# Two graph layers on one core: a shorter grouping, a loop that starts one batch sooner, a new order at the end, and indirect transfers two at a time

## The chip, the cores and the metric

The kernel runs on one core of one Trainium2 chip. The metric is the device time of one execution in microseconds. The kernel before took 1087.72 us in the median of three runs (1087.29 to 1098.17). The profile is of one further execution, which took 1089.15 us; its instructions span 1087.4 us.

## The reference

x is 32 batches of 512 nodes with 512 features, adj a 512 x 512 matrix with about five entries a row, its diagonal set, all values under 1. Everything is float32.

```python
# layer 0
h = relu(layernorm(x))
x = x + einsum('bmd,nm->bnd', h, adj) @ w0 + b0
# layer 1: attention with 8 heads, masked by adj
h = relu(layernorm(x))
q, k, v = h @ Wq + bq, h @ Wk + bk, h @ Wv + bv          # per head of 64
scores = q k^T / 8 + (1 - adj) * -1e9
x = x + softmax(scores) v @ Wo + bo
```

Since every entry of adj is under 1, the mask term is of the order of -1e8 and more, and it leaves one source for each row: the node at which adj is largest in that row. Layer 1 is then, for each row, a fixed linear map of one chosen node's h: z = h[idx] @ (Wv Wo) + (bv Wo + bo), and rows that choose the same node share it. The program tests on the chip that this holds, and has other branches if it doesn't.

## The kernel before, in words

**Preparation.** The first part of `gnn_two_layers` folds Wv and Wo into one matrix, transposes adj, finds each row's chosen node (`idx`), the nodes chosen at all (`used`, 332 of 512 here, so 336 rows are reserved), and computes layer 0's first product of batch 0. Then `single_path` runs.

**A batch.** A batch's rows lie in four chunks of 128 partitions. In iteration b of `run_phase` TensorE computes layer 0's second product of batch b (`layer0`, L632 or L495), then the aggregation of batch b+1, then layer 1's product of batch b-1 (`layer1`, L495). Most products are 2 x 2 block products in the seven-product form (`product`). The iteration has 21 steps: `put(batch, step, f)` hangs a piece of other work on a step, and the pieces of a step are emitted after the step's matmuls and ahead of the evacuation of their result. The order is written out by hand and each engine executes its part in that order. Between layers, h goes to HBM (`put_h`, to hs), comes back with unused rows left out (`get_h`, to hc), and is transposed on VectorE; z goes to HBM (`put_z`), and an indirect transfer with addition (`finish`, L462) gathers it onto x. SyncE's queue carries hs, hc and z. GpSimd's queue carries the indirect transfers.

**Dense and regrouped batches.** Batches up to FIRST = 5 are read in their natural order. Aggregation is a dense 512 x 512 product in the first iterations. In parallel, `Plan` computes an order of the nodes in which the adjacency is sparse by blocks: a quarter of the nodes forms a first block, whose rows may use every source, and the others form three groups of 128. A group's rows may only use sources in the group itself and at most 128 rows from elsewhere, which are gathered once more as "extra rows". `Plan.schedule` spreads this over the dense iterations: `pick_r` chooses the first block, and then each of three rounds counts links (`sources`, `known`, `reach`), scores the nodes (`key_1`, `clip`), ranks them (`rank_pe`) and takes the best into groups (`pick_1`, `pick_2`). `positions`, `place_onehot`, `slots`, `slot_onehot`, `lists` and `indices` turn the groups into index lists (`xi`, `gi`); `rows`, `turn`, `save_at`, `tables`, `tables_g` and `mask_g` rearrange adj; `look_1`, `save_pi`, `look_2`, `packed` make the list by which z is gathered. If no group needs more than 128 extra rows, the flag is set (L893's register test) and the remaining iterations run as the regrouped loop: `spread` in place of the dense aggregation (L608, L611 and L614: 1,280 columns for each of four feature blocks). Else they run dense.

**The regrouped loop on GpSimd's queue.** In iteration b, in this order: `load_x` of batch b+2, four gathers of 128 rows of 2 KB (step 0, L462, `x<-in_x_dram,xi`); `load_g`, three gathers of extra rows (step 4, `at<-in_x_dram,gi`), which wait until ScalarE has read the earlier extra rows; `finish` of batch b-2, four gathers with addition (step 7, `x<-z,pplace`), which wait for z's eight transfers; a memset for `layer1` (L713); and `store` of batch b-2, four scatters (step 14, L479, `out_dram<-x,xi`), each after its own gather has landed. `tc.declare_no_dep` (L484) states that the scatters touch different rows. x has five buffers, so each load waits for the scatter that read its buffer. ScalarE takes the statistics of the extra rows (`NormMore`, L920; the first ones by `lead`, a `NormAct`), VectorE those of x (L361, L362).

**The end.** Batch 31's layer 1 (`layer1_rows`) is computed by rows for all nodes, since nothing is left to overlap. `fetch` reads the z of batches 29 and 30 into free buffers (`sel`, `yT`), `add_z` adds and stores them.

Of the kernel before, what the change touches and what calls it, by code (L numbers as in the profile page):

```python
# [18 lines left out]
P = 128  # L19
# [389 lines left out]
def single_path(ctx: ExitStack, tc: tile.TileContext, x, adj, out, kept, room):  # L409
# [45 lines left out]
    def run_phase(batches, sparse, small, ps_m, ps_t):  # L455
# [4 lines left out]

        def gather(dst, rows, at, **more):
            return nc.gpsimd.indirect_dma_start(out=dst, out_offset=None, in_=rows,  # L462
                                                in_offset=bass.IndirectOffsetOnAxis(ap=at, axis=0), **more)
# [11 lines left out]
        def store_rows(b, c, eng):  # L475
            if natural(b):
                eng.dma_start(out[b, c * P:(c + 1) * P, :], X[b][:, c, :])
                return
            stored = nc.gpsimd.indirect_dma_start(  # L479
                out=out_rows, out_offset=bass.IndirectOffsetOnAxis(ap=plan.xi[:, b, c:c + 1], axis=0),  # L480
                in_=X[b][:, c, :], in_offset=None)
# [197 lines left out]
        def layer1_rows(b):  # L679
            for r in range(C):  # L680
# [7 lines left out]
                nc.vector.tensor_add(x_r, bank.rearrange("p (c q e) -> p q c e", q=4, c=4), x_r)  # L688
                store_rows(b, r, nc.sync)
                for i in range(2):  # L690
                    add_z(B - 3 + r // 2, 2 * (r % 2) + i, nc.sync if r < 2 else nc.scalar)
# [65 lines left out]
        for b in batches:  # L757
            todo = [[] for _ in range(21)]
# [4 lines left out]

            if folded and b == FIRST - 1:
                put(b + 2, 8, load_g)
                for j in range(3):
                    put(b + 2, 12 + j, lambda b, j: lead.stats(j), j)
            if sparse and b == FIRST:
                put(b + 1, 0, lambda b: lead.power())
                put(b + 1, 0, lambda b: lead.offset())  # L770
                for j in range(3):
                    put(b + 1, 1 + j, lambda b, j: lead.relu(j), j)
            if sparse:
                if b > FIRST:
                    put(b + 2, 0, load_x)
                put(b + 2, 4, load_g)
# [6 lines left out]
            put(b - 2, 15 if b == B - 1 else 7 if sparse and b < B else 1, fetch if b > B - 2 else finish)  # L783
            if b < 2:
                put(b + 2, 2 * b, load_x)
            if b > 0 and not sparse:
                put(b + 3, 15, load_x)
# [8 lines left out]
            for c, step in enumerate((1, 3, 9, 12) if b == 0 else (9, 10, 11, 12) if b == B - 2 else (14, 15, 17, 19)):  # L796
                put(b + 1, step, add_b0, c)
            if b < B:
                halves = [norm(X[b], h1_t, [2 * i, 2 * i + 1], Norm if b > 0 or i == 1 else NormAct) for i in range(2)]
# [30 lines left out]
            on_act = b == 0 or folded and not sparse and b < FIRST - 1  # L830
# [32 lines left out]
            if sparse and b == FIRST + 1:  # L863
                put(b, 2, lambda b: plan.look_1())
                put(b, 6, lambda b: plan.save_pi())
                put(b, 15, lambda b: plan.look_2())
# [699 lines left out]
```

## Time and profile before

| | |
|---|---|
| median of three runs | 1087.72 us (1087.29 to 1098.17) |
| profiled execution | 1089.15 us, span 1087.4 us |
| PE busy, weight loads busy | 1011.2 us (93%), 900.0 us (83%) |
| DVE, ACT, POOL busy | 810.1 us (74%), 581.0 us (53%), 564.2 us (52%) |
| software queue (GpSimd's) | 43,984 packets, 118.27 MB, 45.4% of 16 engines |
| hardware queue (SyncE's) | 115,760 packets, 83.37 MB, 30.0% of 16 engines |

How to read it: PE is TensorE, PEld its weight loads, DVE VectorE, ACT ScalarE, POOL GpSimd, SP SyncE. L462 is line 462 of the kernel before. A tile pair such as x<-z,pplace is what an instruction writes and reads. In a timeline, a bracket gives how long the engine was idle before the instruction and what released it; "issue" is a gap that no wait explains. An indirect transfer occupies POOL only while it is issued; the data land later.

The stages, by time in the span: preparation and batch 0 up to 70.93 us; dense iterations 1 to 4, 42.41, 38.90, 41.39 and 40.94 us; the start of the regrouped loop 107.86 us (234.57 to 342.43); 22 batches of the loop 669.68 us; the end 75.29 us.

### The profile page before, as it was taken

The numbers are of one execution on the slowest core, as the hardware profiler recorded it, in microseconds if no ns is written. First come the engines' busy times: TensorE is split into PE (matmuls) and PEld (weight loads), VectorE is DVE, ScalarE is ACT, GpSimd is POOL, SyncE is SP. The second block draws the span as 40 slices with busy tenths as digits, with TensorE's granted clock in tenths as the row PEclk, the third lists the DMA queues.
The fourth block names the chain that finished last, engine by engine and source line by source line (L and its number), as shares of the span: only waits on it lengthen the run. The fifth ranks groups of instructions, "written<-read, shape, count | busy, mean of one in ns | idle before, by whom it ended". The sixth has DMA issues, their size and how long they took to land.

```text
span 1087.4 us, 17059 instructions
## 1 busy us (share of the span) xinstructions
PE 1011.2 (93%) x5672; PEld 900.0 (83%) x5672; DVE 810.1 (74%) x1809; ACT 581.0 (53%) x1266; POOL 564.2 (52%) x659
## 2 busy tenths in 40 slices
PE   8999889978999889999999999999999998999993
PEld 7478778877898878999999988888889888999871
DVE  5897876857787658878777777778777776888762
ACT  3745345255555465566556556665555556666230
POOL 1023216646547435665575575555665565564326
PEclk9999999989899989999999999999999999999997
DMA  9244546968888768888888898988788787987654
GB/s 315 92 85 125 125 111 198 229 193 194 169 207 207 168 178 198 196 201 202 209 219 184 210 232 206 214 196 201 198 207 193 171 213 202 221 197 188 131 169 159
DMA packets 161314, 204.24 MB, mean 188 GB/s; under 512 B 17824, under 2 KB 105632, under 8 KB 161216
## 3 DMA queue, kind: packets, MB, share of 16 engines
q0 software_dynamic: 43984, 118.27, 45.4%
q1 hardware_dynamic: 115760, 83.37, 30.0%
q10 hardware_dynamic: 1472, 1.41, 0.4%
q8 instruction: 47, 0.77, 0.3%
q14 instruction: 51, 0.42, 0.1%
HBM read 120.66 MB, written 82.32 MB: 187 GB/s over the span
## 4 chain that ended last, share of the span: by engine, by line
PE 72%; ACT 4%; DVE 3%; issue 2%; POOL 2%; DMA 1%; another core or an unknown queue 1%; ACTq 0%; POOLq 0%; DVEq 0%
PE mm L495 51%; PE mm L611 11%; PE mm L614 6%; PE mm L608 2%; ACT zs L545 1%; POOL out_dram L479 1%; PE mm L685 1%; DVE st L361 1%; ACT h L379 1%; DMA x<-z,pplace 1%; DVE x L552 0%; DMA at<-in_x_dram,gi 0%; ACT h L394 0%; ACT yT L619 0%
## 5 line engine op out<-in xcount | busy, mean ns | idle before, releaser
L552 DVE TENSOR_TENSOR x<-mm,x 128x512 f32<-128x512 f32 x217 | 148.5, 685 | 130.2 <-PE mm L495 99.3
L379 ACT ACTIVATE h<-x,off,rstd 128x512 f32<-128x512 f32 x256 | 196.5, 807 | 7.8 <-DVE off L370 4.1
L365 ACT ACTIVATE rstd<-mv,eps 128x2 f32<-128x2 f32 (+1 forms) x91 | 26.6, 293 | 300.5 <-DVE mv L362 252.8
L495 PE MATMUL mm<-w_t,sel 128*128 128x256 f32 x744 | 176.1, 386 | 9.5 <-DVE x L552 9.4
L462 POOL DMA_INDIRECT x<-z,pplace x92 | 143.1, 1555 | 72.9 <-DMA z<-zr 37.4
L495 PEld LDWEIGHTS mm<-w_t,sel 128*128 128x128 f32 x744 | 142.1, 192 | 32.2 <-DVE x L552 12.7
L361 DVE BATCH_NORM_STATS2 st<-x 128x6 f32<-128x512 f32 x234 | 157.7, 674 | 1.1
L462 POOL DMA_INDIRECT at<-in_x_dram,gi x78 | 73.9, 948 | 162.0 <-ACT adjT L933 131.6
L495 PE MATMUL mm<-hTs,wvo_t 128*128 128x168 f32 x720 | 122.8, 317 | 32.3 <-ACT zs L545 31.0
L611 PE MATMUL mm<-ap,h 128*128 128x256 f32 x624 | 151.9, 380 | 0.0
L462 POOL DMA_INDIRECT x<-in_x_dram,xi x104 | 111.9, 1076 | 57.4 <-issue 27.1
L495 PEld LDWEIGHTS mm<-hTs,wvo_t 128*128 128x128 f32 x720 | 109.4, 196 | 38.6 <-ACT zs L545 37.3
L479 POOL DMA_INDIRECT out_dram<-x,xi x104 | 108.2, 1040 | 31.2 <-issue 22.0
L545 ACT ACTIVATE zs<-mm,cvo_c 128x168 f32<-128x168 f32 x240 | 82.8, 399 | 68.9 <-PE mm L495 50.9
L611 PEld LDWEIGHTS mm<-ap,h 128*128 128x128 f32 x624 | 110.6, 191 | 10.7
L495 PE MATMUL mm<-w_s,yT 128*128 128x256 f32 x496 | 118.5, 382 | 0.8 <-ACT zs L545 0.8
L495 PEld LDWEIGHTS mm<-w_s,yT 128*128 128x128 f32 x496 | 93.6, 192 | 12.7 <-ACT zs L545 1.0
L614 PEld LDWEIGHTS mm<-ag,adjT 128*128 128x128 f32 x624 | 86.0, 191 | 5.4
L614 PE MATMUL mm<-ag,adjT 128*128 128x128 f32 x624 | 86.4, 275 | 0.0
L586 DVE TENSOR_TENSOR x<-x,b_r 128x512 f32<-128x512 f32 x124 | 84.1, 679 | 0.0
L495 PE MATMUL mm<-hT,wvo 128*128 128x168 f32 x480 | 81.2, 314 | 0.0
L619 ACT COPY yT<-mm 128x512 f32<-128x512 f32 x104 | 59.8, 575 | 38.9 <-PE mm L614 30.3
(314 smaller groups left out, 1703.0 us busy)
## 6 DMA issues: line engine op xcount, KB each, us to landing
hc<-hs SPq DMA_DIRECT2D x124, 176.0 KB
z<-zr SPq DMA_DIRECT2D x120, 96.0 KB
z<-zr SPq DMA_DIRECT2D x120, 80.0 KB
hs<-h SPq DMA_DIRECT2D x50, 192.0 KB
hs<-h SPq DMA_DIRECT2D x50, 160.0 KB
out_dram<-x SPq DMA_DIRECT2D x24, 256.0 KB
x<-in_x_dram SPq DMA_DIRECT2D x16, 256.0 KB
x<-in_x_dram,xi POOLq DMA_INDIRECT x104
```

The costliest lines, as they stand in the source:

```text
L361: self.nc.vector.bn_stats(st, self.src[:, self.chunks[i], :])
L365: self.nc.scalar.activation(self.rstd[:, 0:len(self.chunks)], self.mv[:, :, 1], AF.Sqrt, bias=self.eps)
L379: self.nc.scalar.activation(dst, src, AF.Relu, bias=self.off[:, i:i + 1], scale=self.rstd[:, i:i + 1])
L462: return nc.gpsimd.indirect_dma_start(out=dst, out_offset=None, in_=rows, in_offset=bass.IndirectOffsetOnAxis(ap=at, axis=0), **more)
L479: stored = nc.gpsimd.indirect_dma_start(out=out_rows, out_offset=bass.IndirectOffsetOnAxis(ap=plan.xi[:, b, c:c + 1], axis=0), in_=X[b][:, ...
L495: nc.tensor.matmul(bank[:, m, 0:half], lhs[:, k, m * P:(m + 1) * P], rhs[:, k, :], start=(first and m == 0 and k == 0), stop=(k == 1), ski ...
L545: nc.scalar.activation(dst[:, m, :], bank[:, m, :], AF.Identity, bias=cvo_c[:, 2 * i + m:2 * i + m + 1])
L552: nc.vector.tensor_add(dst, bank, dst)
L586: nc.vector.tensor_add(X[b][:, c, :], X[b][:, c, :], b0_r)
L611: nc.tensor.matmul(two(bank, j), H0[b][:, j, cols], two(plan.ap[:, j, :], j), start=False, stop=False, skip_group_check=True)
L614: nc.tensor.matmul(bank[:, j * P:(j + 1) * P], extra[:, j - 1, cols], plan.ag[:, j - 1, j * P:(j + 1) * P], start=False, stop=(j == C - 1) ...
L619: nc.scalar.copy(yT[:, d, :], bank)
```

## The change

- `Plan.schedule` runs two rounds in place of three; the VectorE half of a count or ranking stands one step behind its TensorE half. The score (`key_1`, `clip`), the starting groups (`constants2`: every third node, in place of thirds of the partitions) and the constants that go with them differ; `positions` and `slot_onehot` are split into parts on several steps.
- FIRST is 4: the regrouped loop begins at iteration 4, and the steps of the plan, `load_g`, `lead` and `load_x` move with it. Plan steps that fall into the loop are issued from `plan.steps` too.
- In dense iterations 0 to 2 half of the second normalization's statistics are taken by ScalarE (`NormAct`).
- In `layer1_rows`, the adds and stores of batch 29 and the fetch of batch 30 come after the first row's product. The adds and stores of batch 30 follow the second and third rows.
- `paced` adds to every indirect transfer that the regrouped loop issues through `gather` and `store_rows`, in iterations below 30, a dependency on the completion of the last but one of them.

```diff
+        moved, pacing = [], [True]
+
+        def paced(move):
+            if sparse and pacing[0]:
+                if len(moved) > 1:
+                    tc.add_manual_dep(move.ins, moved[-2].ins.name, mybir.DependencyInfo(
+                        mybir.DependencyClass.Sync, mybir.DependencyReason.DATA), reason="two at a time")
+                moved.append(move)
+            return move
+
         def gather(dst, rows, at, **more):
-            return nc.gpsimd.indirect_dma_start(out=dst, out_offset=None, in_=rows,
-                                                in_offset=bass.IndirectOffsetOnAxis(ap=at, axis=0), **more)
+            return paced(nc.gpsimd.indirect_dma_start(out=dst, out_offset=None, in_=rows,
+                                                      in_offset=bass.IndirectOffsetOnAxis(ap=at, axis=0), **more))
...
-            stored = nc.gpsimd.indirect_dma_start(
+            stored = paced(nc.gpsimd.indirect_dma_start(
                 out=out_rows, out_offset=bass.IndirectOffsetOnAxis(ap=plan.xi[:, b, c:c + 1], axis=0),
-                in_=X[b][:, c, :], in_offset=None)
+                in_=X[b][:, c, :], in_offset=None))
...
+                if sparse and r == 0:
+                    for c in range(C):
+                        add_z(B - 3, c, nc.sync)
+                    fetch(B - 2)
                 store_rows(b, r, nc.sync)
                 for i in range(2):
-                    add_z(B - 3 + r // 2, 2 * (r % 2) + i, nc.sync if r < 2 else nc.scalar)
+                    if not sparse:
+                        add_z(B - 3 + r // 2, 2 * (r % 2) + i, nc.sync if r < 2 else nc.scalar)
+                    elif 0 < r < C - 1:
+                        add_z(B - 2, 2 * r - 2 + i, nc.sync)
...
+            pacing[0] = b < B - 2
...
             if folded and b == FIRST - 1:
-                put(b + 2, 8, load_g)
+                put(b + 2, 16, load_g)
+            if sparse and b == FIRST:
                 for j in range(3):
-                    put(b + 2, 12 + j, lambda b, j: lead.stats(j), j)
-            if sparse and b == FIRST:
-                put(b + 1, 0, lambda b: lead.power())
-                put(b + 1, 0, lambda b: lead.offset())
+                    put(b + 1, j, lambda b, j: lead.stats(j), j)
+                put(b + 1, 3, lambda b: lead.power())
+                put(b + 1, 3, lambda b: lead.offset())
                 for j in range(3):
-                    put(b + 1, 1 + j, lambda b, j: lead.relu(j), j)
+                    put(b + 1, 4 + j // 2, lambda b, j: lead.relu(j), j)
...
-                put(b + 2, 4, load_g)
+                put(b + 2, 6 if b == FIRST else 4, load_g)
...
+            on_act = b == 0 or folded and not sparse and b < FIRST - 1
             if b < B:
-                halves = [norm(X[b], h1_t, [2 * i, 2 * i + 1], Norm if b > 0 or i == 1 else NormAct) for i in range(2)]
+                halves = [norm(X[b], h1_t, [2 * i, 2 * i + 1], NormAct if i == 0 and (b == 0 or on_act) else Norm)
+                          for i in range(2)]
...
-FIRST = 5
+FIRST = 4
...
-        v.tensor_scalar(self.ind[:, 0:1], self.pp, 42.5, None, op0=ALU.is_lt)
-        v.tensor_scalar(self.ind[:, 2:3], self.pp, 85.5, None, op0=ALU.is_gt)
-        v.tensor_add(self.ind[:, 1:2], self.ind[:, 0:1], self.ind[:, 2:3])
-        v.tensor_scalar(self.ind[:, 1:2], self.ind[:, 1:2], -1.0, 1.0, op0=ALU.mult, op1=ALU.add)
+        for j in range(3):
+            v.tensor_reduce(self.ind[:, j:j + 1], self.kept["ident"][:, j::3], AX.X, ALU.add)
...
-        v.tensor_tensor(s, self.ps, self.ub, ALU.add)
-        v.scalar_tensor_tensor(s, s, 2.0, self.L[:, :, 0:3], op0=ALU.mult, op1=ALU.subtract)
+        v.scalar_tensor_tensor(s, self.ub, 1.5, self.ps, op0=ALU.mult, op1=ALU.add)
...
-        for r in range(3):
-            for gap, kind, f in ((0, pe, self.sources), (0, at, self.known), (3, pe, self.reach), (0, at, self.key_1),
-                                 (3, pe, self.rank_pe), (0, at, self.pick_1), (3, pe, self.rank_pe),
-                                 (0, at, self.pick_2), (3, None, None)):
-                k += gap
-                if f:
-                    kind(*divmod(k, 21), f)
+        for r in range(2):
+            for go, then in ((self.sources, self.known), (self.reach, self.key_1), (self.rank_pe, self.pick_1),
+                             (self.rank_pe, self.pick_2)):
+                pe(*divmod(k, 21), go)
+                at(*divmod(k + 1, 21), then)
+                k += 3
...
+        at(2, 18, self.rows)
+        at(2, 20, self.look_1)
         for m in range(4):
-            pe(*divmod(k + 10 + m, 21), self.turn, m)
-        at(*divmod(k + 12, 21), self.save_at, 0)
-        at(*divmod(k + 14, 21), self.save_at, 2)
-        at(3, 20, self.tables)
-        at(4, 0, self.tables_g)
-        at(4, 11, self.mask_g)
+            pe(3, 4 + m, self.turn, m)
+        at(3, 6, self.save_at, 0)
+        at(3, 8, self.save_at, 2)
+        at(3, 8, self.save_pi)
+        at(3, 12, self.tables)
+        at(3, 14, self.tables_g)
+        at(4, 0, self.mask_g)
+        at(4, 10, self.look_2)
+        at(5, 8, self.packed)
```

## The prediction

> **What bounds the kernel now.** I read the stretches of the profile first (columns: window, its length, then busy time and instruction count of PE, PEld, DVE, ACT and POOL, granted clock, DMA share, GB/s), to find the period of a batch in each stage.
>
> ```profile
> 113.34:152.24 38.90, 36.09 (x254) 31.70 (x253) 32.32 (x96) 17.10 (x39) 11.00 (x13) 1.00 0.59 146
> 193.63:234.57 40.94, 34.98 (x170) 31.57 (x168) 28.55 (x60) 16.22 (x37) 25.27 (x27) 0.92 0.86 219
> ...
> 342.43:1012.11 669.68, 644.47 (x3698) 593.18 (x3697) 513.05 (x1101) 395.03 (x858) 393.58 (x435) 0.99 0.84 199
> 1012.11:1087.40 75.29, 53.20 (x273) 41.95 (x271) 39.50 (x78) 16.72 (x36) 31.49 (x48) 0.91 0.55 161
> ...
> 530.91:559.76 28.85, 28.85 (x169) 26.67 (x168) 23.30 (x51) 17.90 (x39) 20.00 (x22) 1.00 0.83 215
> ```
>
> The first two are dense batches (2 and 4): 39 to 41 us each. The third is 22 batches of the regrouped loop, from the first L608 matmul of batch 8 to that of batch 30: 669.68/22 = 30.44 us each. The last is one undisturbed batch: TensorE has no gap, so 28.85 us is its floor, and 1.6 us a batch is lost on average to gaps. In the loop TensorE is the bound, with little to spare for a second bound.
>
> Next the queues, and then POOL's instructions over one undisturbed batch (start, us, what, idle before).
>
> ```profile
> q0 software_dynamic: 43984, 118.27, 45.4%
> q1 hardware_dynamic: 115760, 83.37, 30.0%
> ```
> ```profile
> 529.95 1.59 POOL L462 DMA_INDIRECT x<-z,pplace  x1 [3.89 <-DMA z<-zr]
> 531.85 1.55 POOL L462 DMA_INDIRECT x<-z,pplace  x1 [0.30 <-issue]
> ...
> 537.42 1.07 POOL L479 DMA_INDIRECT out_dram<-x,xi  x1 [0.17 <-issue]
> 538.79 1.04 POOL L479 DMA_INDIRECT out_dram<-x,xi  x1 [0.19 <-issue]
> ...
> 543.20 1.80 POOL L479 DMA_INDIRECT out_dram<-x,xi  x1 [1.98 <-DMA x<-z,pplace]
> 545.30 1.16 POOL L462 DMA_INDIRECT x<-in_x_dram,xi  x1 [0.19 <-issue]
> 546.76 0.96 POOL L462 DMA_INDIRECT x<-in_x_dram,xi  x1 [0.30 <-issue]
> ...
> 551.03 0.94 POOL L462 DMA_INDIRECT at<-in_x_dram,gi  x1 [0.80 <-issue]
> ...
> 557.06 1.59 POOL L462 DMA_INDIRECT x<-z,pplace  x1 [2.26 <-DMA z<-zr]
> ```
>
> A batch is fifteen indirect transfers in POOL's order: four accumulates (F, from z), four stores (S), four loads of x (X), three loads of extra rows (G). Within a train they start 1.3 us apart (F: 1.86), which is what issuing costs. POOL waits for almost nothing, yet from one F to the next takes 27 of the 28.85 us. The transfers are deep in flight: the trace's packet records close each one with sixteen 4-byte packets (7,456 for 466 transfers), and taking the last of each sixteen, in order of issue, as the landing, the last but one had not landed when the next was issued for 100% of the S, 94% of the X, 67% of the F and 53% of the G in the loop. This is exactly what the change forbids.
>
> [...] G with nothing in flight takes 3.25, F 4.57[...] X landings are 0.9 to 1.3 us apart when SP's queue is quiet, 2.5 to 4.1 beside its hc reads. [...]
>
> **The change, part by part.** *One round fewer.* A round is two counts (sixteen small matmuls, 0.54 us each) and two rankings (0.55 each): 2.2 us of PE, on the path. Its DVE operations (rows of 0.16 to 0.29 us) sum to about 5 us, part of them in DVE's idle time. Moving half of the norm statistics of batches 1 and 2 to ACT takes 1.7 us (two of 0.67 plus 0.18) off DVE in each; ACT has room (17 of 39 us). PE's gaps in batches 1 to 3 (122.7 us together, 110.4 busy) can shrink but not vanish: I take 8 us off, between 2 and 14. Whether two rounds still give a usable plan I worked out in plain arithmetic on the reference's adjacency: the three groups need 124, 114 and 123 outside rows (limit 128), against 113, 123 and 111 after three. So the regrouped branch is taken.
>
> *The loop one batch sooner.* Dense batch 4 (40.94 us, with a stretch at a lower granted clock and 5.2 us in which PE waits behind ACT's statistics of the first extra rows) goes; one more loop batch comes. The statistics of the first extra rows move from that dense batch into the first loop batch, five steps before they are needed; the start of the loop (batch 5's layer 0 to batch 8's first L608) took 107.86 us and I keep that. Position tables, gathers and saves move one to 1.5 batches earlier, in batches where POOL is busy 11 of 39 us: nothing.
>
> *The end.* POOL idles 5.33 us before the yT fetches (1054.85 to 1060.18) and then runs twelve stores back to back to 1080.84. Four of these stores (batch 29) now fill that idle time from about 1057.9, when their adds are done: sixteen issues of 1.28 us from there end at 1078.3, so 2.5 us less. The adds that now stand behind the first row's on DVE wait for sel (landed 1057.87) before the second row's product is ready (1061): no cost.
>
> *The wait.* It is on POOL, so everything behind it on POOL waits too: the memset that layer 1's z needs, and the next transfers, in order. SP and ACT queues are not behind it. In the built order of the changed kernel every F, X and G and the first two S of a batch wait for the last but one; the third and fourth S don't, since stores are declared free of each other. The last loop batches (from 30) and the end are not paced. No row of before shows the wait at this place, so I price it. Landing to restart: 0.26 us from semaphore to start, and 0.24 to 1.6 (median 0.65) from the last packet to the semaphore, at the existing waits for S and F: 0.9. Issue to landing with at most one other in flight: F 4.57 to 4.69 (30 cases), G 3.25 to 3.81 (31), X 4.42 (only 4 cases; shortest of all 3.2), S not seen so (shortest 2.82, with more in flight 4.65 to 4.93). I take F 4.65, S 3.0, X 3.8, G 3.6. Two tokens then alternate over the odd number of transfers:
> F1, F3, S1, two issue steps to S3, X1, X3, G1, G3, next F2: 2 x 5.55 + 2 x 1.3 + 3.9 + 2 x 4.7 + 2 x 4.5 = 36.0;
> F2, F4, S2, two steps to S4, X2, X4, G2, next F1: 11.1 + 2.6 + 3.9 + 9.4 + 4.5 = 31.5.
> The mean, 33.75 us a batch, is above TensorE's 28.85 and above 30.44: POOL becomes the bound, DVE's statistics wait for x and ACT's for the extra rows. Bounds: with each shortest value (F 4.36, S 2.5, X 3.15, G 3.12, restart 0.7) the chain is 29.3, which would be a gain; with each long one (4.9, 3.5, 4.6, 4.0, 1.1) 38.3. Paced batches 5 and 6 carry no indirect stores and stay under TensorE's floor, so 23 batches (7 to 29) pay.
>
> *Sum*, on the profiled execution (span 1087.4, whole 1089.15). Start to batch 1: 70.9. Batches 1 to 3: 114.7. To batch 7's first L608: 107.9. 23 x 33.75 = 776.3. From batch 30's on: 75.3 - 2.5 = 72.8. Span 1142.6, plus 1.75 around it 1144.3; the profiled execution stands 1.4 above the median of before (1087.72), so **1143 us**, +5.1%.
>
> **The rivals.** *The wait is covered (faster).* Fewer transfers in flight land sooner, SP's 10.2 us a batch (30.0% of 1087.4 over 32) goes through undisturbed, and POOL's chain fits in TensorE's period. Then the other parts show: 366.3 + 23 x 28.82 to 30.44 is 1029 to 1066; I take 1045. For it: gaps before L495 in most batches from 618 to 925, X that lands in 3.2 us even now. Against it: it needs short values everywhere. It decides at a chain of (1087.4 - 366.3)/23 = 31.35 us. *Level.* Quiet values (F 4.5, S 2.6, X 3.2, G 3.25, restart 0.9) give 31.3 a batch: 1087. *Crowded.* If q1's transfers stretch most paced transfers as they do X now, the chain passes 36: 1195 or more. *The change doesn't do what it says.* If the plan on the chip exceeds the limit, all 28 later batches run dense at some 35.5: about 1240.
>
> **How the numbers follow.** Forecast (chain 31.8 to 36) 0.62; covered 0.15; level 0.08; crowded 0.11; dense 0.04. A measurement of this kernel can tell about 1% from no change. Faster 0.15, same 0.08, slower 0.77. The range runs from inside the covered case, 1060, to inside the crowded one, 1205: about 0.08 is left out below and 0.11 above.
>
> **What would show it.** Right: in POOL's timeline pairs of transfers with idle time before each, ended by DMAs of its own queue; a loop period of 32 to 36; BATCH_NORM waiting for x<-in_x_dram on DVE, the row sums (L920 before) waiting for at<-in_x_dram on ACT; q0's and q1's bytes as before but a lower DMA share. The dense part ends near 186, the last store 2 to 3 us closer to the last matmul. Wrong: a loop period under 31 with POOL idle between trains. The restart price and X's landing, seen in few cases, are what I trust least.

## The result

The kernel after takes 1198.64 us in the median of four runs (1192.69 to 1199.77), the kernel before, measured beside it, 1087.51. The ratio is 1.099, with a 95% interval of 1.091 to 1.107. A second set of runs gave 1196.12 us and 1.099 (1.092 to 1.106). The profiled execution took 1198.81 us with a span of 1196.8.

The stretches of the profile after (window, its length, busy time and count of PE, PEld, DVE, ACT and POOL, granted clock, DMA share, GB/s) are a dense batch, the stretch from layer 0 of batch 4 to the first regrouped aggregation, 21 paced batches, the end from batch 30's first L618 on, and one paced batch:

```profile
110.95:146.49 35.54, 35.04 (x234) 30.88 (x233) 31.82 (x90) 19.74 (x48) 14.13 (x16) 1.00 0.71 117
191.11:213.55 22.44, 17.01 (x56) 13.87 (x57) 7.52 (x15) 6.91 (x16) 9.01 (x10) 0.78 0.62 182
...
336.46:1088.08 751.62, 656.68 (x3530) 592.17 (x3528) 484.67 (x1051) 375.45 (x819) 379.65 (x422) 0.93 0.70 172
...
1122.79:1196.80 74.01, 53.21 (x273) 41.96 (x271) 39.63 (x78) 16.72 (x36) 33.38 (x48) 0.91 0.58 165
589.07:624.16 35.09, 30.77 (x169) 27.86 (x168) 23.07 (x51) 17.89 (x39) 17.87 (x20) 0.95 0.69 171
```

751.62/21 = 35.79 us a paced batch, where before had 30.44. In the single batch PE is busy 30.77 us, not 28.85, so it is idle for 4.3 us and slower in the rest (granted clock 0.95, where before's batch had 1.00). The loss lies here: from batch 7's spread to batch 30's 815.15 us pass (307.64 to 1122.79), 35.44 for each of 23.

The DMA queues of the page after:

```profile
q0 software_dynamic: 44544, 120.10, 42.3%
q1 hardware_dynamic: 115024, 81.99, 25.8%
```

The bytes differ by under 2% from before, since one more batch is regrouped. q0's packets took 506 us of the span (42.3% of 1196.8) instead of 494, q1's 309 instead of 326. The transfers themselves hardly changed; what changed is when they start. F, S, X and G stand for accumulates, stores, loads of x and loads of extra rows, as in the prediction, numbered in POOL's order. POOL's timeline after (start, us, what, idle before and what ended it), one batch from its second accumulate to the next batch's second:

```profile
602.29 1.55 POOL L472 DMA_INDIRECT x<-z,pplace  x1 [0.31 <-issue]
607.12 1.53 POOL L472 DMA_INDIRECT x<-z,pplace  x1 [3.27 <-DMA x<-z,pplace]
609.23 1.53 POOL L472 DMA_INDIRECT x<-z,pplace  x1 [0.58 <-DMA x<-z,pplace]
610.20 0.73 POOL L730 MEMSET zs<- 128x64 f32 x1
...
614.76 1.00 POOL L489 DMA_INDIRECT out_dram<-x,xi  x1 [1.36 <-DMA x<-z,pplace]
...
616.07 0.96 POOL L489 DMA_INDIRECT out_dram<-x,xi  x1 [0.19 <-issue]
...
620.98 0.98 POOL L472 DMA_INDIRECT x<-in_x_dram,xi  x1 [2.57 <-DMA out_dram<-x,xi]
...
624.82 0.95 POOL L472 DMA_INDIRECT x<-in_x_dram,xi  x1 [1.20 <-DMA x<-in_x_dram,xi]
...
628.88 0.95 POOL L472 DMA_INDIRECT at<-in_x_dram,gi  x1 [1.76 <-DMA x<-in_x_dram,xi]
...
633.62 0.95 POOL L472 DMA_INDIRECT at<-in_x_dram,gi  x1 [2.32 <-DMA hs<-h]
...
638.64 1.64 POOL L472 DMA_INDIRECT x<-z,pplace  x1 [0.30 <-issue]
```

Read the starts as a path: F2 602.29, F4 609.23, S2 614.76, S3 616.07, X1 620.98, X3 624.82, G1 628.88, G3 633.62, F2 again at 638.64. Every step but the issue step from S2 to S3 is the landing of the last but one and a restart (at G3 the label of the idle time names another transfer; by the packet records it started 1.2 us after G1 had landed. F2 came 1.7 us after G3's landing, since F1, issued 2.2 us before it, stood ahead of it.) Before, POOL issued these trains in steps of 1.3 us (accumulates 1.9). In the listing of the kernel after an accumulate keeps POOL 1.5 to 1.6 us, and the others 0.95 to 1.0; by the packet records the accumulates of this stretch land 4.6 to 6.4 us after their start, the others 2.9 to 5.4.

The waits after, in the window 336 to 1088 (who waits at which line for whom: us in total, times, longest):

```profile
DVE zr L735 <- POOL zs L730: 118.2, 21, 6.9
...
PE mm L505 <- DVE x L562: 93.0, 21, 5.7
...
POOL x L472 <- DMA x<-z,pplace: 78.6, 38, 4.0
POOL x L472 <- DMA out_dram<-x,xi: 58.2, 26, 3.5
POOL out_dram L489 <- DMA x<-z,pplace: 49.3, 39, 2.2
```

Once in each of the 21 batches TensorE waits some 4.4 us for the adds of layer 0. How it gets there is seen in the timeline of all engines around 610 us:

```profile
607.53 1.89 PE L505 MATMUL mm<-w_t,sel 128*128 128x256 f32 x8
...
610.96 0.85 DVE L735 STREAM_TRANSPOSE zr<-zs 128x640 f32<-128x640 f32 x1 [5.52 <-POOL zs L730]
...
613.03 1.25 DVE L562 TENSOR_TENSOR x<-mm,x 128x512 f32<-128x512 f32 x2
613.74 3.45 PE L505 MATMUL mm<-w_t,sel 128*128 128x256 f32 x8 [4.32 <-DVE x L562]
```

The memset of zs (L730) stands on POOL behind the paced accumulates and runs at 610.20. VectorE's transposes of zs (L735) wait for it 5.52 us, the adds of layer 0 (L562) stand behind them on VectorE, and TensorE's third block product (the piece u2 of `product`) behind the first add. Then eight matmuls take 3.45 us that took 1.89 at 607.53; the granted clock was 0.55 in these 3.45 us, and 1.00 from 607.53 to 609.42.

### The profile page after: what moved, and what is told of

It reads as the page before. It is cut to its first block, busy times and chain, and to the rows that moved or that the text cites. A ratio compares the mean times of both kernels' runs of the same rounds, so it can differ in the third digit from the quotient of the medians.

```text
span 1196.8 us, 16975 instructions
## 1 busy us (share of the span) xinstructions
PE 1050.3 (88%) x5624; PEld 923.7 (77%) x5624; DVE 796.8 (67%) x1779; ACT 585.5 (49%) x1282; POOL 566.7 (47%) x666
## 3 DMA queue, kind: packets, MB, share of 16 engines
q0 software_dynamic: 44544, 120.10, 42.3%
## 4 chain that ended last, share of the span: by engine, by line
PE 36%; DMA 30%; DVE 17%; POOL 7%; issue 5%; ACT 3%; another core or an unknown queue 0%; ACTq 0%; POOLq 0%; SPq 0%; DVEq 0%
PE mm L505 29%; DMA x<-z,pplace 14%; DMA at<-in_x_dram,gi 10%; POOL x L472 5%; DVE st L361 4%; DVE x L562 3%; DVE zr L735 3%; ACT h L379 2%; DVE hT L722 2%; DMA x<-in_x_dram,xi 2%; PE mm L621 2%; PE mm L271 1%; POOL out_dram L489 1%; DVE mv L362 1%; PE mm L150 1%
## 5 line engine op out<-in xcount | busy, mean ns | idle before, releaser
L505 PE MATMUL mm<-w_t,sel 128*128 128x256 f32 x744 | 213.4, 439 | 108.1 <-DVE x L562 107.8
L505 PEld LDWEIGHTS mm<-w_t,sel 128*128 128x128 f32 x744 | 159.2, 218 | 144.3 <-DVE x L562 118.6
L562 DVE TENSOR_TENSOR x<-mm,x 128x512 f32<-128x512 f32 x217 | 145.9, 681 | 181.4 <-PE mm L505 131.7
L472 POOL DMA_INDIRECT x<-z,pplace x96 | 158.6, 1652 | 139.3 <-DMA x<-z,pplace 87.2
L472 POOL DMA_INDIRECT x<-in_x_dram,xi x108 | 104.8, 970 | 138.1 <-DMA out_dram<-x,xi 59.4
L621 PE MATMUL mm<-ap,h 128*128 128x256 f32 x648 | 157.7, 380 | 0.0
L735 DVE STREAM_TRANSPOSE zr<-zs 128x640 f32<-128x640 f32 (+1 forms) x60 | 54.7, 911 | 132.5 <-POOL zs L730 126.8
L505 PE MATMUL mm<-w_s,yT 128*128 128x256 f32 x496 | 136.2, 424 | 4.9 <-ACT zs L555 4.9
L472 POOL DMA_INDIRECT at<-in_x_dram,gi x81 | 79.0, 975 | 113.7 <-DMA x<-in_x_dram,xi 24.9
L505 PEld LDWEIGHTS mm<-w_s,yT 128*128 128x128 f32 x496 | 109.8, 224 | 24.4 <-ACT zs L555 5.1
L505 PE MATMUL mm<-hTs,wvo_t 128*128 128x168 f32 x720 | 114.0, 307 | 3.7 <-ACT zs L555 3.0
L596 DVE TENSOR_TENSOR x<-x,b_r 128x512 f32<-128x512 f32 x124 | 84.1, 679 | 0.0
```

The lines of the kernel that those rows point to most:

```text
L472: return paced(nc.gpsimd.indirect_dma_start(out=dst, out_offset=None, in_=rows, in_offset=bass.IndirectOffsetOnAxis(ap=at, axis=0), **more))
L505: nc.tensor.matmul(bank[:, m, 0:half], lhs[:, k, m * P:(m + 1) * P], rhs[:, k, :], start=(first and m == 0 and k == 0), stop=(k == 1), ski ...
L562: nc.vector.tensor_add(dst, bank, dst)
L596: nc.vector.tensor_add(X[b][:, c, :], X[b][:, c, :], b0_r)
L621: nc.tensor.matmul(two(bank, j), H0[b][:, j, cols], two(plan.ap[:, j, :], j), start=False, stop=False, skip_group_check=True)
L735: nc.vector.transpose(zr[:, s0:s1, :].rearrange("p s (c e) -> p s c e", c=4), zt(b)[:, :, 32 * s0:32 * s1].rearrange("p c (s j) -> p s c j ...
```

## Experiments

The main theory: a chain of landings and restarts on POOL is the period, and it reaches TensorE wherever it meets it first. The rival: the memset behind the accumulates is the link, and the chain itself has room. A second question is where the gain of the other parts went.

Landings below are read as in the prediction (the last of sixteen 4-byte packets, in order of issue), and starts of batches from the first L618 matmul (L608 in before).

### The wait left out, and put into the kernel before

```diff
-            if sparse and pacing[0]:
+            if False:
```

> The kernel after, with the wait for the last but one transfer left out everywhere; all else of the change stays. Theory (the wait alone makes the loss, and the chain of POOL's transfers is the period): the loop returns to before's 28.8 to 30.4 us a batch, 23 x 28.82 to 30.44 = 663 to 700; with a loop start at 299 to 308 us (307.6 in the profile after; its paced first batches cost up to 8.7 of it) and an end of 73 to 74: 1037 to 1084 whole, most likely 1065, a gain on before. Rival (the earlier start of the loop costs too, about as much as it saves): 1085 or more, same as before.

1069.05 us (1059.42 to 1082.53), before 1075.07 beside it: 0.992 (0.989 to 0.995). Its loop (window from batch 7's spread to batch 30's):

```profile
305.40:982.80 677.40, 666.20 (x3866) 614.58 (x3865) 534.32 (x1152) 410.08 (x897) 416.58 (x456) 1.00 0.84 206
```

29.45 us each of 23: the loop is back at before's rate or better. It is 138 us shorter than with the wait, in the profiled execution, which was the fastest of twenty (1059.42 us); in the median up to 10 us of this are missing. The start of the loop stays late (batch 7's spread at 305.4, after 307.6), so that cost is not the wait's. What the other parts bring together is 0.8%.

The wait alone, on the same transfers of the kernel before (`gather` and `store_rows` through `paced`, nothing else changed):

> The kernel before, with the wait alone put in, on the same transfers. Theory (costs add): 22 or 23 paced batches at 35.4 to 35.8 us in place of 30.44, so +110 to +123: 1197 to 1211, at or above the kernel after. Rival (the wait is dear only with the loop started early, where plan gathers and loads lie together): clearly under 1180.

1203.59 us against 1075.07: 1.118 (1.112 to 1.124). Its loop, 22 batches:

```profile
341.40:1128.40 787.00, 685.43 (x3697) 618.57 (x3696) 509.91 (x1104) 393.09 (x858) 397.41 (x440) 0.93 0.70 172
```

35.77 us each, as in the kernel after. Together: the wait alone makes the loss, and it makes the same period in both kernels.

### The memset taken off POOL

```diff
-                nc.gpsimd.memset(zt(b)[:, :, room:32 * S], 0.0)
+                nc.vector.memset(zt(b)[:, :, room:32 * S], 0.0)
```

> The kernel after, wait included, with the memset of zs (L730), which stands behind the last paced accumulate on POOL, given to VectorE. Theory (the chain of POOL's transfers is the period, the memset only the place where TensorE meets it): nothing to gain, 1190 to 1205, TensorE's idle time of some 4.5 us a batch ends in another wait (for x or for hT). Rival (the memset is the link): TensorE's 107.8 us of waits behind x at L562 go, and with them the stretches of half clock: 1080 to 1105.

1211.87 us, 1.130 (1.123 to 1.136): no gain, and 7 us over the theory's range; from batch 7's spread (304.6 us) to batch 30's (1129.4) 35.86 us a batch. The waits of this kernel in the window 336 to 1088:

```profile
ACT adjT L934 <- DMA at<-in_x_dram,gi: 115.7, 24, 8.0
...
PE mm L505 <- ACT zs L555: 103.1, 21, 7.2
...
DVE st L361 <- DMA x<-in_x_dram,xi: 62.5, 59, 2.8
```

The wait on the memset is gone, and in its place stand the ones that the prediction named: ScalarE's row sums wait for the extra rows, VectorE's statistics for the loads of x. ScalarE's copies of zs stand behind the row sums, and TensorE behind these, 103.1 us over 21 batches where it was 93.0. So the memset was the place, not the cause of the loss. But the equal period is here the sum of other terms. Accumulates of this kernel also waited for VectorE (30.2 us for its adds at L596 alone; the first of a batch started 1.7 us after the landing of the last but one, where it was 0.65 in the kernel after), while stores landed in 2.4 to 3.4 us where they took 3.6 to 4.1. That POOL's chain needs no other engine is seen in the kernel after, where each step of the path but the issue step is a landing and a restart (0.55 to 1.3 us in the batch shown, 1.7 ahead of F2, where F1 stood in between).

### One, three and four in flight

```diff
-                if len(moved) > 1:
-                    tc.add_manual_dep(move.ins, moved[-2].ins.name, ...
+                if len(moved) > 2:
+                    tc.add_manual_dep(move.ins, moved[-3].ins.name, ...
```

(and `> 0` with `moved[-1]`, `> 3` with `moved[-4]`).

> The kernel after, each transfer waiting for the last one. Theory (a chain of landings and restarts on POOL sets the period): fifteen landings and restarts in a row with the values measured after, less the stores that are free of each other, give 67 us a batch; 60 if a transfer alone lands as soon as the shortest now do. 23 batches at 60 to 67 us: 1760 to 1930 whole. Rival (TensorE's stalls by the memset and by half clock set it, which do not scale with the chain): under 1500.

1750.87 us in the one run, below the range by 0.5%. The window of the last twenty batches of the loop:

```profile
526.20:1676.10 1149.90, 676.25 (x3362) 611.23 (x3361) 467.71 (x1002) 357.28 (x780) 354.37 (x403) 0.77 0.45 107
```

57.5 us each. The miss is small: with nothing else of POOL's in flight but the free stores, landings are shorter than assumed, namely accumulates 4.5 to 4.8 us, loads of x 3.1 to 3.6, extra rows 2.9 to 3.3. The chain sets the period here too.

> The kernel after, each transfer waiting for the last but two in place of the last but one. Theory (a chain of landings and restarts): with the landing times measured after (accumulates 4.6 to 6.3 us, stores 3.6 to 4.1, loads of x 3.0 to 3.3, extra rows 3.2 to 4.1, restart 0.6 to 1.3) a batch of fifteen transfers takes 25 us with three in flight, 28 us if each lands 0.7 us later: under TensorE's 28.8, so the loss goes entirely, 1055 to 1085, within 1% of the kernel without the wait. Rival (each wait has a price of its own on POOL, or the memory needs four or five in flight): the loop stays above 32 us a batch, 1120 to 1150.

1049.48 us (1039.5 to 1055.0), before 1075.07: 0.978 (0.972 to 0.985). That is under the theory's range (1055 to 1085), faster than both kernels, and than the kernel without the wait on the same chip (0.992). The loop, and one of its batches:

```profile
299.10:963.80 664.70, 663.33 (x3865) 615.20 (x3864) 535.71 (x1151) 410.75 (x897) 413.26 (x455) 1.00 0.85 210
...
530.50:559.30 28.80, 28.80 (x170) 26.73 (x169) 23.28 (x51) 17.89 (x39) 18.27 (x20) 1.00 0.87 213
```

28.90 us each of 23, PE busy 663.33 of 664.70: TensorE's floor. (The profiled execution was the fastest of the four; in the median at most 10 us of gaps come back.) The whole loss of the wait for the last but one is gone with one more transfer in flight, as the chain (25 to 28 us against 28.8) had it. Why three in flight also beat no wait by 20 us on this chip was not shown.

> The kernel after, each transfer waiting for the last but three, so four in flight. Theory (the wait costs nothing once its chain, 22 us a batch with four in flight, lies under TensorE's 28.8, and what it gains is that loads are held off the small transfers): where before's loop has stalls, a part of the gain of three in flight stays, ratio to before 0.975 to 0.99; where before has none (1042 us) 0.995 to 1.0. Rival (only three in flight or fewer holds anything back): the kernel without the wait, 0.99 or more where before has stalls.

1065.33 us, before 1074.75: 0.989 (0.983 to 0.996), where the theory said 0.975 to 0.99 and the rival 0.99 or more: the interval covers both. The kernel without the wait had 0.992, on another chip. The loop has stalls again:

```profile
305.20:992.00 686.80, 670.51 (x3866) 618.52 (x3865) 534.92 (x1152) 411.72 (x897) 411.58 (x454) 1.00 0.85 203
```

29.86 us each. What four in flight hold back can't be told from no wait.

Does three in flight help by itself?

> The kernel before with the wait alone put in, for the last but two. Theory (three in flight keep the loads off the backs of the small transfers, and the gain does not need the other parts of the change): the loop goes from about 30 us to 28.8 to 29.2 a batch, ratio to before 0.980 to 0.990. Rival (the gain of three in flight needs the regrouped loop's earlier start): 0.995 or more.

No: 1041.81 us against 1041.91, 1.0005 (0.999 to 1.002). On this chip the kernel before itself took 1041.91 us, where it took 1087.51, 1075.07, 1090.51 and 1074.75 beside the other sets. So the theory's number was missed and the rival's came, but the run does not decide between them. The reason is in the denominator: there was nothing to gain there, since this kernel's loop runs at TensorE's floor (634.20 us for 22 batches, 28.83 each, shown below) and before is no slower. Three in flight took away stalls where there were some (the kernel after, 0.978 against 0.992); it did not make a loop without stalls faster. The kernel before with three in flight was not run on a chip on which before has stalls, so whether they go there without the other parts stays open. Why these stalls differ from set to set was not tried either; each chip was measured once.

### The path through the chain

```diff
-            stored = paced(nc.gpsimd.indirect_dma_start(
+            stored = nc.gpsimd.indirect_dma_start(
...
-                in_=X[b][:, c, :], in_offset=None))
+                in_=X[b][:, c, :], in_offset=None)
```

> The kernel after, with the stores of rows left out of the wait: they neither wait for the last but one nor are counted; accumulates, loads of x and extra rows still are. Theory (the period is the longest path through landings and restarts): with the values measured after, eleven transfers two at a time and four stores issued at once give 31.4 us a batch (35.5 with the stores counted): 23 batches give back 94 us, 1104 whole, between 1075 and 1140 for 30.1 to 33. Rival (the accumulates and the stalls behind them set the pace alone, and the stores were mostly free of it already): at least 34.5 us a batch, 1175 or more.

1153.85 us (1148.66 to 1155.84), before 1090.51: 1.058 (1.051 to 1.066). The kernel after beside it:

> The kernel after, unchanged, beside the others on one chip. Every theory: 35 to 36 us a batch whatever the kernel before does there, 1190 to 1205; where before runs at 1042 the ratio is then 1.14 to 1.16 in place of 1.10.

1196.12 us, before 1090.51: 1.099; the expected ratio for a chip on which before takes 1042 was not put to the test. Freeing the stores gives back 42 us, and 46.5 in the loop. The loops, first of the kernel with free stores, then of the kernel after:

```profile
311.70:1080.40 768.70, 701.06 (x3865) 636.26 (x3864) 532.53 (x1154) 411.01 (x897) 411.05 (x457) 0.95 0.74 183
```

```profile
306.20:1121.40 815.20, 715.36 (x3865) 645.88 (x3865) 532.18 (x1153) 410.70 (x897) 413.95 (x459) 0.93 0.71 172
```

33.42 us a batch against 35.44: between theory (31.4, at most 33) and rival (34.5 or more), and the whole time outside the range of both. The missing term is the landing of the loads of x: beside four stores in flight the first two land in 4.6 us, not in the 3.1 that the kernel after showed. With this kernel's own landings and restarts the path is F2 to F4 6.85, five issue steps to X1 6.7, X1 to X3 6.04, to G1 4.17, to G3 4.18, to the next F2 4.88: 32.8 of the 33.4. Starts of one engine always add up to its period; what speaks for the path is that each of these steps, but for the issue steps, is the landing of the transfer waited for and a restart of 0.6 to 1.5 us. So the path stands, but landings may not be carried from one spacing to another.

### The start and the end

Two kernels with three in flight, both run beside a before of 1041.91 us, differ only in the other parts of the change: `before_last_but_two` (above) and the kernel after with the old end.

```diff
-                if sparse and r == 0:
-                    for c in range(C):
-                        add_z(B - 3, c, nc.sync)
-                    fetch(B - 2)
                 store_rows(b, r, nc.sync)
                 for i in range(2):
-                    if not sparse:
-                        add_z(B - 3 + r // 2, 2 * (r % 2) + i, nc.sync if r < 2 else nc.scalar)
-                    elif 0 < r < C - 1:
-                        add_z(B - 2, 2 * r - 2 + i, nc.sync)
+                    add_z(B - 3 + r // 2, 2 * (r % 2) + i, nc.sync if r < 2 else nc.scalar)
...
-            if not (sparse and b == B):
-                put(b - 2, 15 if b == B - 1 else 7 if sparse else 1, fetch if b > B - 2 else finish)
+            put(b - 2, 15 if b == B - 1 else 7 if sparse and b < B else 1, fetch if b > B - 2 else finish)
```

> The kernel after with three transfers in flight, and the end in before's order (adds and stores of the last three batches by rows of the last product, the fetch in the step before). Theory (twelve stores in a row on POOL close the end; four of them moved into its idle time save two issue steps): 2 to 3 us longer from the last batch's spread to the end, 76 in place of 73.7 us; ratio to before 0.978 to 0.983. Rival (the end is set by the last row's chain of matmul, add and store, wherever the other stores stand): the same within 1 us.

1039.86 us, 0.998 (0.997 to 1.000) against 1041.91. The end came as expected (75.7 us, below), the ratio did not, since before has no stalls on this chip. The stretches of `before_last_but_two`: dense batches 1 to 3, dense batch 4, batch 5 to batch 8's spread, 22 batches, the end:

```profile
71.33:190.10 118.77, 110.16 (x721) 95.92 (x720) 95.27 (x255) 54.89 (x123) 40.91 (x53) 0.99 0.59 150
190.10:231.12 41.02, 35.28 (x170) 31.88 (x169) 28.57 (x60) 16.21 (x37) 25.28 (x27) 0.92 0.86 219
231.12:330.70 99.58, 98.93 (x561) 91.04 (x562) 77.81 (x171) 56.19 (x121) 55.84 (x55) 1.00 0.82 199
330.70:964.90 634.20, 634.20 (x3698) 588.63 (x3697) 512.56 (x1101) 393.61 (x858) 395.42 (x436) 1.00 0.85 211
964.90:1039.50 74.60, 53.18 (x273) 41.93 (x271) 39.67 (x78) 16.71 (x36) 32.33 (x48) 0.89 0.56 163
```

And of the kernel after with three in flight and the old end: dense batches 1 to 3, batch 4 to batch 7's spread, 23 batches, the end:

```profile
71.26:183.13 111.87, 107.44 (x673) 94.42 (x671) 90.55 (x231) 55.92 (x125) 49.27 (x60) 0.98 0.75 154
183.13:298.90 115.77, 103.59 (x560) 93.47 (x561) 78.96 (x175) 60.38 (x133) 63.12 (x64) 0.94 0.81 208
298.90:961.80 662.90, 662.90 (x3866) 615.38 (x3865) 536.12 (x1152) 411.50 (x897) 414.38 (x456) 1.00 0.85 210
961.80:1037.50 75.70, 53.19 (x273) 41.93 (x271) 39.80 (x78) 16.73 (x36) 31.89 (x48) 0.88 0.54 160
```

The grouping with two rounds saves 6.9 us in batches 1 to 3. (Over all profiles the middle is 122.7 us in three with three rounds, and 115.8 in eleven with two. But batch 3 alone took 39.6 to 44.6 us in eight profiles of kernels that share its code, and 58.3 in a ninth, that of the kernel with free stores, so a few us in the start of one profile can be chance.) The dense batch 4 saves 41.0 and one more loop batch costs 28.8; but the first three regrouped batches take 115.8 us where they took 99.6, 16.2 more. Of 19 us that the earlier start should save, 3 are left (41.0 + 6.9 - 28.8 - 16.2). Between the kernels before and after themselves the three batches differ by less, 107.9 and 116.5 us.

TensorE loses 8 to 10 of these 16 us in batch 4. In the kernel after the timeline shows who is late:

```profile
195.02 0.29 DVE L1269 TENSOR_SCALAR ag<-ag,valid 128x128 f32<-128x128 f32 x1 [2.89 <-issue]
...
201.24 0.63 ACT L394 ACTIVATE ph<-at 128x512 bf16<-128x512 f32 x1 [10.19 <-DMA at<-in_x_dram,gi]
...
201.81 3.78 PE L505 MATMUL mm<-w_t,sel 128*128 128x256 f32 x8 [5.43 <-DVE x L562]
```

VectorE masks the rows of ag when their gather lands (by the packet records at 194.0, 195.7 and 196.6 us), with the adds of layer 0 behind it; ScalarE waits for the first extra rows. So the mask was moved:

```diff
-        at(4, 0, self.mask_g)
+        at(4, 5, self.mask_g)
```

> The kernel after with three transfers in flight (each waits for the last but two), and the masking of the gathered rows of ag (L1269, three VectorE operations) moved from step 0 to step 5 of batch 4. Theory (at the first regrouped batch TensorE loses its 5 to 8 us because VectorE stands at this masking, waiting for the gather of ag, with the adds of layer 0 behind it): the gap between the first and second w_s,yT products of batch 4 falls from 15.5 us to 5 to 8, and 5 to 9 us of the whole go: ratio to before 0.970 to 0.974 (three in flight without it: 0.978). Rival (something else holds VectorE there, as the 3.4 us that it stands idle after the masking in the kernel after suggest): the gap stays over 12 us and the time the same, 0.976 to 0.981.

1037.28 us, 0.997 (0.995 to 0.998) against 1041.91. The gap between the two w_s,yT products of batch 4 (the first and the fourth of layer 0's seven) fell from 15.4 us (198.54 - 183.13 with the old end) to 5.3, but the wait came back later in the same batch:

```profile
198.95 0.63 ACT L394 ACTIVATE ph<-at 128x512 bf16<-128x512 f32 x1 [14.18 <-DMA at<-in_x_dram,gi]
203.79 0.18 DVE L404 RECIPROCAL rstd<-rstd 128x3 f32<-128x3 f32 x1 [12.79 <-ACT rstd L401]
...
205.42 0.80 PE L505 MATMUL mm<-w_t,yT 128*128 128x256 f32 x1 [9.97 <-DVE x L562]
```

The statistics of the first extra rows are the second barrier: VectorE's reciprocal waits for ScalarE, ScalarE for rows that land from 197.9 us on. From batch 1's layer 0 to batch 7's spread this kernel takes 226.3 us (299.1 - 72.8), the one with the old end 227.6: 1.3 us gained, not 5 to 9. It began batch 1 1.5 us later, so its lead over the old end (span 1034.9 against 1037.5) is made by the end:

```profile
961.90:1034.90 73.00, 53.23 (x273) 41.95 (x272) 39.92 (x78) 16.71 (x36) 34.50 (x48) 0.91 0.58 169
```

73.0 us with the new end, 75.7 with the old: 2.7. Between the two kernels that differ in the end alone, run on different chips, it is 2.0 (73.7, the last but two). But the same end varies between profiles: the old one took 74.6 to 75.8 us in four, the new one 73.0 to 74.8 in ten. The means are 1.6 us apart.

The other barrier was then attacked as well, by fetching the extra rows earlier:

```diff
-                put(b + 2, 16, load_g)
+                put(b + 2, 14, load_g)
```

> Three transfers in flight (the last but two), the masking of ag (L1269) at step 5 of batch 4, and the first extra rows (load_g of batch 5) fetched two steps earlier in batch 3, ahead of the gathers of ag and of the loads of x on POOL's queue. Theory (TensorE's 10 us of idle time in batch 4 are the statistics of the first extra rows: VectorE's reciprocal L404 stands behind ScalarE, which waits for these rows, which land eighth of ten in a row at 198.6 us): they land some 9 us sooner, the idle time falls to under 4 us, and 5 to 8 us go: span 1027 to 1031 where it was 1034.9 with the masking moved alone; ratio to before 0.988 to 0.993 where before has no stalls in its loop (1042 us), less where it has. Rival (another landing, of ag or of x, takes its place): within 2 us of the kernel with the masking moved alone.

1054.98 us, before 1090.51 beside it: 0.969 (0.963 to 0.976), the lowest ratio of all, though on a chip on which before is slow, and so no proof that it beats the kernels above. The start did not get shorter: from batch 1's layer 0 to batch 7's spread 237.3 us, where the kernel after and the one with free stores took 234.7 and 239.4 beside it. The extra rows landed from 194.1 to 197.3 us, but those of ag behind them from 197.9 to 199.2, and TensorE still waits 6.4 us ahead of the first product of batch 4 and 3.3 at the third. Batch 3 takes 46.5 us (147.5 to 194.0, between first w_s,yT products) where the kernel with the mask alone moved had 39.8 (145.0 to 184.8); given how batch 3 varies, not all of this need come from the move. The landings fit the rival, in which another one takes the place of the one moved; the profile names no releaser for the 6.4 us, so that it is this one is not shown. All these gathers stand in one row on POOL's queue with the saves and loads of batch 3, and neither order of theirs that was tried ends the waiting.

## Why the prediction was right or wrong

The direction and the engine were right: slower, with POOL as the bound, 1198.6 us inside 1060 to 1205. The size was not: +5.1% was forecast, +9.9% measured, and 1143 was 56 us short. The forecast's own chain of up to 36 us ends at 1195, so the result lies in the range by the room that was left for the crowded case, whose mechanism did not occur: in that much the range was lucky. On the profiled execution (1196.8 against the sum of 1142.6) the 54 us lie as follows.

- **Loop, 23 x 33.75 = 776.3: measured 815.15, 38.9 too low.** The step that failed is the mean over two alternating chains (36.0 and 31.5). The first was put down as "F1, F3, S1, two issue steps to S3". But S2 stands between, with its own wait for F4, which waits for F2. So S3 follows F2, F4, S2 in every batch, and both chains run through it: nothing alternates, the longer path is the period. With the prediction's own values that path (F2, F4, S2, S3, X1, X3, G1, G3, F2) is 2 x 5.55 + 1.3 + 3.9 + 2 x 4.7 + 2 x 4.5 = 34.7, 0.95 more in each of 23 batches: 22 us. The rest is the size of terms, 35.74 for 34.7 in the 22 batches that were held: accumulates landed in 4.6 to 6.3 us (5.4 in the mean) where 4.65 was taken, stores in 3.6 to 4.1 (3.0, an estimate; the last twelve stores of before landed in 2.35 to 3.1), extra rows in 3.2 to 4.1 (3.6), while loads of x took 3.0 to 3.3 (3.8) and restarts mostly 0.6 to 1.2 (0.9). With the means of these the path is about 35.6. Batch 7 itself was not yet held (28.82 us), 5.9 us to the other side.
- **Start to batch 7, 293.5: measured 307.6.** Batches 1 to 3 took 119.5 us for 114.7 (115.1 in the second profiled execution of the same kernel, 115.8 in the middle of all with two rounds), so the 8 us off 122.7 were about right, though this execution shows only 3. What failed is "position tables, gathers and saves move one to 1.5 batches earlier: nothing" and that the loop's start keeps its 107.9 us. It took 116.5, and in before's form it ran in 99.6 in one kernel. The moved gathers and statistics are on queues that were counted as idle, but VectorE's mask and the adds behind it wait for the rows of ag (landed 194.0 to 196.6 us in the kernel after), and ScalarE waited 10.19 us for the first extra rows.
- **End, 72.8: measured 74.0.** The 2.5 us off were 1.3 here and 1.6 between the means of all profiles with the old and the new end: right in kind, too large.
- **How POOL reaches TensorE.** Named were VectorE's statistics of x and ScalarE's sums. In the kernel after the statistics of x wait for no load in the loop, and the row sums for extra rows 3.9 us in all, so these two signs did not come. They held TensorE up only with the memset off POOL. The list of what is queued behind the waiting instruction had the memset in it; that VectorE's transposes, the adds and TensorE hang on it was not followed up. For the time it made no difference that could be seen: with the memset moved the period was the same.
- **The rivals.** Covered (1045) and level (1087) failed at two in flight, but covered is what three in flight does. Crowded had the time (1195 or more) by the wrong mechanism: the loads of x landed sooner (3.0 to 3.3 us where 3.8 was taken), not later. The regrouped branch was taken, as the plain arithmetic had it.
- **The signs.** Pairs with idle time ended by POOL's own DMAs, a period of 32 to 36 us and lower DMA shares came as written; the dense part ended at 191.1 us (186.6 in the second execution) for 186.

## What to carry to other kernels

Here the wait on POOL, whose transfers start in order, made a chain of landings. Its period was the longest path, so draw the paths through every transfer that has a second predecessor before taking a mean, and compare with the floor of the engine that bounds: two in flight made 35 us against a floor of 28.8, three made 28.9 and cost nothing. What is moved earlier for the sake of time counts with what waits for it in order (ScalarE 10.19 us for the first extra rows), not with the load of its queue. And a loop that loses time in one chip's profile may lose none on the next (before had medians of 1042 to 1091 us in five sets): compare only beside a run of the old kernel.

## What was not expected of the hardware

- After gaps of 4.32 and 5.43 us in TensorE the next eight matmuls took 3.45 and 3.78 us, where they take 1.89. The clock record of the kernel after grants half for 3.41 us from 614.1 us on, and the granted clock was 0.50 from 201.81 to 205.59. In the window 336 to 1088 TensorE stood idle for 3.15 to 5.74 us ahead of the third block product once in each of the 21 batches, and each time the record grants half for one stretch of 3.41 or 6.83 us beside the restart. The prediction left this out. PE was busy 30.77 us in the held batch shown (granted clock 0.95), where the loop with three in flight and the old end has 28.82 a batch (662.90/23, clock 1.00); the granted clock was 0.93 over the 21 batches, and 0.77 with one in flight. That this lengthens the period was not shown: each step of POOL's path but the issue step is a landing and a restart.
- How long a transfer took to land differed with what else was under way. By the packet records of the loops (means by place in the train), with one, two, three in flight and without the wait: accumulates 4.5 to 4.8, 4.6 to 6.3, 4.6 to 6.2, 4.7 to 6.2 us; loads of x 3.1 to 3.6, 3.0 to 3.3, 4.0 to 5.1, 4.3 to 6.2; extra rows 2.9 to 3.3, 3.2 to 4.1, 3.2 to 3.5, 4.2 to 4.7. The number in flight is not all: with two in flight stores took 3.6 to 4.1 us in the kernel after, and 2.4 to 3.4 with the memset moved. From landing to restart took 0.6 to 1.0 us ahead of accumulates, stores and the third and fourth load of x with two in flight, and 1.1 to 1.2 ahead of the first load of x and of extra rows.
- The same kernel before ran at medians of 1042 to 1091 us in the five sets, while the kernel after had medians of 1198.64 and 1196.12 beside 1087.5 and 1090.5, and before with the wait 1203.59 beside 1075: so the held loop hardly follows the chip in these. What it takes on a chip on which before takes 1042 was not seen.
